# Layernorm's input for rows 1 to 3 loaded already transposed, in place of transposes on TensorE

## The chip, the cores and the metric

The kernel runs on one core of a Trainium2 chip. The metric is the device time of one execution in microseconds (us). Engines are named as in the profile: PE is TensorE (PEld its weight loads), DVE VectorE, ACT ScalarE, POOL GpSimd, and SP the engine that here only issues DMAs.

## The reference

Input x has 4 rows of 512 tokens with 1024 values each, in float32.

```python
xn = _layernorm(x)                                # (x - mean) / sqrt(var + 1e-5) over the 1024 values
q, k, v = xn @ Wq, xn @ Wk, xn @ Wv               # 16 heads of 64; rotary embedding on q and k
attn = softmax(where(causal, q @ k.T, -1e9) / sqrt(64))
s = (attn @ v) @ Wo
routing = softmax(xn @ gate_w.T, axis=1)          # 8 experts
out = (xn * (routing @ in_scale)) @ sign(weight).T * (routing @ out_scale) + bias
return x + s * silu(out)
```

## The kernel before

**Stages.** The first 770 us or so are attention; then come the output projection, the gated layer and the end. Attention works on 16 groups k = (b, g): row b of four, group g of four, a group being two units (u0 and u1) of two heads each. Groups 0 to 3 are row 0. While the softmax of one group runs, the projections of the next fill TensorE: the planning loop (L889 to L953) makes 16 `pieces` for each group, and `interleave` (L880) issues a piece and then its share of 84 projection matmuls. A float32 matmul has two records in the profile.

**Projections** take the transposed, normalized row X[b] (128 values of E by 8 chunks by 512 tokens). They follow Strassen's scheme: sums of quarters of the weights (S1 to S4, `form_w`, L288) and of X (T1 to T4, `form_x`, L311, once per row, at the end of g=3 and before its next row) are made on VectorE, seven products go through a ring of four PSUM banks (L125), and are added up on VectorE (c, v, part) and, for one term, on GpSimd (part, L388).

**One unit's chain** (names as in the profile): projection c; ScalarE swaps halves into sw (L319, L320, four instructions of 32 partitions for each of q and k), VectorE makes rot (L321), GpSimd multiplies sw by the sine (L322) and adds it to rot (L323). TensorE makes the scores sc (L525); VectorE masks and takes the maximum (L545, L548), ScalarE makes p by exp with the sum (L551), VectorE the reciprocal rs (L559), and GpSimd multiplies p by rs (L561), in eight pieces of 128, 256, 384 and 512 columns, the 128 ones last. `transpose_blocks` (L569) turns p in 32x32 blocks on VectorE (y, ten instructions, L579) and 16 DMAs on SP's queue move the blocks back to p (L589). TensorE makes the values pv (L604), and ScalarE copies them out of a bank of the ring to v (L613); a store to at_d follows (L617).

**Order.** TensorE's order is written out by hand (`manual_schedule(engines={PE})`, L61). The other engines' orders come from the tile framework's scheduler when the kernel is built, except where `tc.keep_in_program_order` fixes one; on the chip each engine takes its instructions in that order, and one that waits holds all behind it.

**Layernorm of rows 1 to 3 (b+1 while row b runs).** A row has four tiles t of 128 tokens, with tokens on partitions. `load_x` (L156) loads a tile of 512 KB: tiles 0 and 1 at piece 11 of g=1, 2 and 3 at pieces 11 and 15 of g=2. `half_statistics` (L166), `deviation` (L174) and `normalize` (L182) run at the start and at piece 3 of g=2 (tiles 0, 1) and g=3 (tiles 2, 3): two instructions of statistics (L171), their aggregate, the root on ScalarE, the reciprocal, and (x - mean) * rstd in one VectorE instruction (L187). `transpose_x` (L194) then transposes a half tile with four matmuls on TensorE (L200) at pieces 7, 8, 13 and 14, and copies the bank into X[b+1], the first half on VectorE (L204), the second on ScalarE (L206); a store of the tile to xn_d follows (L210), which the gated layer reads later. Row 0 does the same before the first group. Signs of the gated layer's weights are loaded and made (`load_sign`, `make_sign`, L679 and L706) in groups k = 5, 9, 12 and 14.

Of the kernel before, what the change touches and what calls it, by code (L numbers as in the profile page):

```python
# [9 lines left out]
F32 = mybir.dt.float32  # L10
F32R = mybir.dt.float32r
AF = mybir.ActivationFunctionType
ALU = mybir.AluOpType
# [7 lines left out]
B, S, E = 4, 512, 1024  # L21
H, D = 16, 64
NE = 8
P = 128
NT = B * S
NC = E // P
NPAIR = H // 2
NGRP = NPAIR // 2
TPB = S // P
# [13 lines left out]
def attn_gated_ffn_kernel(  # L43
    ctx: ExitStack,
    tc: tile.TileContext,
    x: bass.AP,
    wqk: bass.AP,
    wv: bass.AP,
    wo: bass.AP,
# [9 lines left out]
    nc = tc.nc  # L59
# [37 lines left out]
    for sign, base in ((1, 0), (-1, 7)):  # L97
        nc.gpsimd.affine_select(
            out=high,
            in_=high,  # L100
            compare_op=ALU.is_ge,
            fill=0.0,
            base=base,
            pattern=[[-16 * sign, 8]],
            channel_multiplier=sign,
        )
    row_kind = cp.tile([P, 3], F32, name="row_kind")


# [1 line left out]
    xn_d = dp.tile([B, TPB, P, E], F32, name="xn_d")  # L111
    at_d = dp.tile([B, TPB, P, E], F32, name="at_d")

    rt_d = dp.tile([B, TPB, 32, P], F32, name="rt_d")

    sg = {n: sgp.tile([P, E], F32R, name=f"sg{n}") for n in range(NC - 1)}
# [39 lines left out]
    def load_x(b, t):  # L156
        if b == 0:
            xt = X1[:, t, :]
        else:
            xt = xip.tile([P, E], F32, tag="x", name=f"x_{b}_{t}")  # L160
        nc.sync.dma_start(out=xt, in_=x[(b * TPB + t) * P : (b * TPB + t + 1) * P, :])
        xin[b, t] = xt
# [11 lines left out]
    def deviation(b, t):  # L174
        stats = BN[b, t]
        mv = st.tile([P, 2], F32, tag="mv", name=f"mv_{b}_{t}")
        nc.vector.bn_aggr(mv, stats)
        std = st.tile([P, 1], F32, tag="std", name=f"std_{b}_{t}")
        nc.scalar.activation(std, mv[:, 1:2], AF.Sqrt, bias=eps)
        MV[b, t] = mv, std  # L180

    def normalize(b, t):  # L182
        xt = xin[b, t]
        mv, std = MV[b, t]
        rstd = st.tile([P, 1], F32, tag="rstd", name=f"rstd_{b}_{t}")
        nc.vector.reciprocal(rstd, std)
        nc.vector.tensor_scalar(xt, xt, mv[:, 0:1], rstd, op0=ALU.subtract, op1=ALU.mult)  # L187

    def layernorm_scales(b, t):
        half_statistics(b, t, 0)  # L190
        half_statistics(b, t, 1)
        deviation(b, t)

    def transpose_x(b, t, g):  # L194
        if b not in X:
            X[b] = xp.tile([P, NC, S], F32, tag="X", name=f"X_{b}")
        tp = tp_bank(f"xtp_{b}_{t}_{g}")
        for j in range(4):
            c = 4 * g + j
            nc.tensor.transpose(tp[:, j, :], xin[b, t][:, c * P : (c + 1) * P], ident)  # L200
        dst = X[b][:, 4 * g : 4 * g + 4, t * P : (t + 1) * P]

        if (g == 0 and b > 0) or (g == 1 and (b, t) == (0, TPB - 1)):
            nc.vector.tensor_copy(dst, tp)  # L204
        else:
            nc.scalar.copy(dst, tp)  # L206
        if g == 1:

            queue = nc.scalar if (b, t) == (B - 1, TPB - 1) else nc.sync
            queue.dma_start(  # L210
                out=xn_d[b, t].rearrange("p (c q) -> p c q", c=NC),
                in_=X[b][:, :, t * P : (t + 1) * P],
            )
# [474 lines left out]
    def split_scales(dst):  # L688
        v = scales.pop(0)
        h, low, sign = (row_kind[:, n : n + 1] for n in range(3))  # L690
        pin = tc.keep_in_program_order
        if not scales_done:
            pin(nc.vector.tensor_reduce(h, high, AX.X, ALU.max))
            pin(nc.vector.tensor_scalar(low, h, -1.0, 1.0, op0=ALU.mult, op1=ALU.add))
            pin(nc.vector.tensor_scalar(sign, h, 2.0, -1.0, op0=ALU.mult, op1=ALU.add))
        scales_done.append(dst)

        pin(nc.vector.tensor_copy(dst, v))
        pin(nc.vector.tensor_scalar(v, v, low, None, op0=ALU.mult))
        pin(  # L700
            nc.vector.scalar_tensor_tensor(
                dst, dst.bitcast(F32), sign, v, op0=ALU.mult, op1=ALU.add
            )
        )
# [185 lines left out]
    for k, (b, g) in enumerate(groups):  # L890
        pieces = [[] for _ in range(9)]
        if k > 0:
            pieces, late = attention_pieces(k - 1, late)

        def at(n, piece):
            pieces[n].append(piece)


        if g == 0:
            routing = [lambda n=n: router(b, n) for n in range(3)]  # L900
            if k == 0:
                at(0, routing[0])
                at(1, lambda: (load_scales(in_scale), load_scales(out_scale)))
                at(2, routing[1])
                at(4, routing[2])
                at(5, lambda: split_scales(isc))
            else:
                if b < B - 1:
                    at(5, routing[0])
                at(8, routing[1])  # L910
                at(15, routing[2])
        elif g == 1 and b + 1 < B:

            at(11, lambda: [load_x(b + 1, t) for t in range(2)])
            if b == 0:
                at(1, lambda: split_scales(osc))
        elif g > 1 and b + 1 < B:
            t0 = 2 * (g - 2)

            layernorm_scales(b + 1, t0)  # L920
            layernorm_scales(b + 1, t0 + 1)
            normalize(b + 1, t0)
            at(3, lambda: normalize(b + 1, t0 + 1))
            for n, t, h in ((7, t0, 0), (8, t0, 1), (13, t0 + 1, 0), (14, t0 + 1, 1)):
                at(n, lambda t=t, h=h: transpose_x(b + 1, t, h))
            if g == 2:
                at(11, lambda: load_x(b + 1, 2))
                at(15, lambda: load_x(b + 1, 3))
        if k in (5, 9, 12, 14):
            n = {5: 0, 9: 2, 12: 4, 14: 6}[k]  # L930
            at(0, lambda: (load_sign(n), load_sign(n + 1)))
            at(8, lambda: make_sign(n))
            at(15, lambda: make_sign(n + 1))
        if b == B - 1:

            if g < 2:
                load_xn(g)
            if g in (1, 2):
                at(1, lambda: in_scales(g - 1, score_banks))
            if g == 3:  # L940
                z_place[0] = [xip.tile([P, E], F32, tag="x", name=f"z0_{i}") for i in range(2)]
                at(1, lambda: out_scales(0, score_banks))
        if k == 11:

            at(15, lambda: router(b + 1, 0))
        interleave(pieces, fill, 3 * 7 * 4 if k else 3 * 7 * 4 - 8)
        if g == NGRP - 1:
            for _ in fill:
                pass
            if b + 1 < B:  # L950
                for n in (3, 1, 2, 4) if b + 1 < B - 1 else (3, 2, 4, 1):
                    form_x(b + 1, n)
                fill = projections(b + 1)  # L953
# [473 lines left out]
```

## Time and profile before

| | |
|---|---|
| three runs | 1108.65, 1109.48, 1110.82 us; median 1109.48 |
| span of the profiled execution | 1108.7 us |
| granted TensorE clock, first slice to last | 0.9 or more of full speed in each of 40 |
| DMA | 163.88 MB, mean 148 GB/s |
| group starts of row 0 (g=0 to 3) | 12.5, 50.2, 92.5, 141.7 us |
| group starts of row 1 | 190.2, 238.8, 285.6, 335.6 us |
| group starts of row 2 | 383.7, 432.4, 479.1, 529.9 us |
| group starts of row 3, and their end | 578.0, 630.5, 677.2, 725.9; 772.5 us |

The groups' starts are read from the timeline of TensorE. The profile shows one execution. In a line of the groups, "out<-in" are tile names without their numbers, then the partitions and elements, the count, the busy time in us and the mean of one in ns; after the bar comes the idle time of the engine just before these instructions, and what ended most of it. A line of the timeline has start and duration in us, the engine, the line of code, the operation and how many of them; in brackets the idle time before it and who ended it. The view of waits adds up the idle time of an engine by what it waited for.

### The profile page before, as it was taken

How to read it: one execution, taken by the hardware profiler on the slowest of the kernel's cores; microseconds unless marked ns; L12 is line 12 of the kernel's file. 1: busy time of each engine (PE TensorE's matmuls, PEld its weight loads, DVE VectorE, ACT ScalarE, POOL GpSimd, SP SyncE). 2: the span in 40 equal slices, each digit the busy share in tenths (PEclk: the TensorE clock that was granted, in tenths of full speed). 3: DMA queues.
4: the chain of work that ended last, by engine and by line, in shares of the span. 5: the costliest groups of instructions: out<-in, count | busy, mean ns of one | idle time of the engine just before them, and what ended most of it. 6: DMA issues, size and time to landing. Idle time of an engine off the chain costs nothing. (4 is left out here: it accounts for less than half of the span.)

```text
span 1108.7 us, 15895 instructions
## 1 busy us (share of the span) xinstructions
PE 1087.4 (98%) x5176; PEld 790.2 (71%) x5176; DVE 870.4 (79%) x1740; ACT 461.3 (42%) x1072; POOL 518.9 (47%) x566
## 2 busy tenths in 40 slices
PE   9999999999999999999999999999999999999997
PEld 8887778777777877777788687777664545654663
DVE  7888888788988978888887887887776877567663
ACT  2452754453375445427544452655530223122220
POOL 0772645555264555526453562675552433432334
PEclk9999999999999999999999999999999999999999
DMA  9415566544556654455666445544664222431331
GB/s 323 135 69 147 149 184 189 160 137 119 166 155 187 190 154 135 121 163 158 184 183 219 140 148 142 153 125 122 179 193 171 90 93 102 148 119 54 136 114 57
DMA packets 86770, 163.88 MB, mean 148 GB/s; under 512 B 13472, under 2 KB 49056, under 8 KB 80672
## 3 DMA queue, kind: packets, MB, share of 16 engines
q1 hardware_dynamic: 80144, 152.25, 46.1%
q0 software_dynamic: 4832, 9.05, 2.4%
q10 hardware_dynamic: 1712, 1.57, 0.5%
q8 instruction: 41, 0.67, 0.3%
q14 instruction: 41, 0.34, 0.1%
HBM read 95.45 MB, written 25.43 MB: 109 GB/s over the span
## 5 line engine op out<-in xcount | busy, mean ns | idle before, releaser
L561 POOL TENSOR_SCALAR p<-p,rs 128x256 f32<-128x256 f32 (+3 forms) x256 | 183.7, 734 | 200.6 <-DVE rs L559 136.2
L551 ACT ACTIVATE p<-sc,nmx 128x256 f32<-128x256 f32 (+3 forms) x256 | 132.9, 529 | 104.8 <-DVE nmx L548 87.2
L338 PE MATMUL pj<-X,w 128*128 128x256 f32 x576 | 134.3, 382 | 1.7 <-ACT p L551 1.5
L338 PE MATMUL pj<-T,S 128*128 128x256 f32 x512 | 120.5, 385 | 8.5 <-ACT v L613 8.5
L579 DVE STREAM_TRANSPOSE y<-p 128x256 f32<-128x256 f32 x320 | 112.4, 409 | 18.3 <-POOL p L561 16.9
L322 POOL TENSOR_TENSOR sw<-sw,sin_sb 128x512 f32<-128x512 f32 x64 | 85.1, 1330 | 81.1 <-ACT sw L320 75.4
L338 PEld LDWEIGHTS pj<-X,w 128*128 128x128 f32 x576 | 108.1, 190 | 20.0 <-issue 2.9
L338 PEld LDWEIGHTS pj<-T,S 128*128 128x128 f32 x512 | 96.7, 192 | 24.8 <-ACT v L613 11.3
L319 ACT ACTIVATE sw<-c 32x512 f32<-32x512 f32 x128 | 80.3, 628 | 70.0 <-DVE c L352 68.2
L338 PE MATMUL pj<-T,w 128*128 128x256 f32 x448 | 106.6, 382 | 0.0
L548 DVE TENSOR_REDUCE nmx<-sc 128x1 f32<-128x256 f32 (+3 forms) x160 | 105.2, 683 | 1.3
L425 PE MATMUL pj<-w,X 128*128 128x256 f32 x416 | 94.6, 380 | 0.8 <-ACT p L551 0.5
L338 PEld LDWEIGHTS pj<-T,w 128*128 128x128 f32 x448 | 83.4, 190 | 15.5 <-issue 4.6
L323 POOL TENSOR_TENSOR rot<-rot,sw 128x512 f32<-128x512 f32 x64 | 90.8, 1419 | 5.0
L425 PEld LDWEIGHTS pj<-w,X 128*128 128x128 f32 x416 | 78.2, 190 | 12.7 <-ACT p L551 2.0
L545 DVE TENSOR_TENSOR sc<-sc,mask 128x256 f32<-128x256 f32 (+1 forms) x160 | 57.0, 371 | 35.3 <-PE sc L525 35.3
L320 ACT ACTIVATE sw<-c 32x512 f32<-32x512 f32 x128 | 80.4, 628 | 1.6
L425 PE MATMUL pj<-w,T 128*128 128x256 f32 x352 | 80.2, 381 | 0.0
L525 PE MATMUL sc<-rot,rot 64*128 64x128 f32 (+3 forms) x512 | 79.7, 443 | 0.3 <-DVE v L451 0.3
L604 PE MATMUL pv<-p,v 128*64 128x256 f32 (+3 forms) x512 | 76.0, 439 | 0.4 <-issue 0.4
L388 POOL TENSOR_TENSOR part<-part,part 128x256 f32<-128x256 f32 x32 | 24.7, 771 | 105.2 <-ACT part L387 102.0
L613 ACT COPY v<-pv 128x512 f32<-128x512 f32 x32 | 18.7, 585 | 131.5 <-PE pv L604 131.4
(177 smaller groups left out, 1956.9 us busy)
## 6 DMA issues: line engine op xcount, KB each, us to landing
p<-y SPq DMA_DIRECT2D x496, 80.0 KB, 2.1
w<-in_wqk SPq DMA_DIRECT2D x31, 1024.0 KB, 5.3
w<-in_wv SPq DMA_DIRECT2D x16, 1024.0 KB, 5.2
x<-in_x SPq DMA_DIRECT2D x16, 512.0 KB, 4.3
at_d<-v SPq DMA_DIRECT2D x32, 256.0 KB, 2.7
xp<-xn_d SPq DMA_DIRECT2D x16, 512.0 KB, 4.6
ap<-at_d SPq DMA_DIRECT2D x16, 512.0 KB, 5.1
xr<-in_x SPq DMA_DIRECT2D x32, 256.0 KB, 3.0
```

What stands on the lines that cost most here:

```text
L319: nc.scalar.activation(sw[r : r + 32, :], c[r + 32 : r + 64, :], AF.Copy, scale=sc)
L320: nc.scalar.activation(sw[r + 32 : r + 64, :], c[r : r + 32, :], AF.Copy, scale=sc)
L322: nc.gpsimd.tensor_tensor(sw, sw, sin_sb, op=ALU.mult)
L323: nc.gpsimd.tensor_tensor(rot, rot, sw, op=ALU.add)
L338: nc.tensor.matmul(ps, lhsT=wq[:, k, :], rhs=xq[:, k, :], start=(k == 0), stop=(k == 3))
L425: nc.tensor.matmul(ps[:, j, :], lhsT=xq[:, k, j * P : (j + 1) * P], rhs=wq[:, k, :], start=(k == 0), stop=(k == 3),)
L525: nc.tensor.matmul(head(i, h), lhsT=Q[u][r : r + D, i * P : (i + 1) * P], rhs=K[u][r : r + D, : (i + 1) * P], start=True, stop=True,)
L548: nc.vector.tensor_reduce(nmx[:, hs], v, AX.X, ALU.max, negate=True)
L551: nc.scalar.activation(pt[:, h, :], ps[h], AF.Exp, bias=nmx[:, h : h + 1], accum_out=ssum[:, h : h + 1],)
L561: nc.gpsimd.tensor_scalar(pt[:, h, :], pt[:, h, :], rs[:, h : h + 1], 1.0, op0=ALU.mult, op1=ALU.mult,)
L579: nc.vector.transpose(out[:, :, :, o : o + 32], src.rearrange("p h (b c) -> p h b c", b=4))
L604: nc.tensor.matmul(by_block[r : r + D, :, 32 * j :], lhsT=V[u][:, j, r : r + D], rhs=PT[u][:, :, o : o + 32 * (TPB - j)], start=(j == 0), ...
```

## The change

A second input xT holds x transposed on the host: for each row 128 values by 8 chunks by 512 tokens. For rows 1 to 3, X[b+1] is loaded from it straight into place, in four DMAs of 512 KB: two at piece 11 of g=1 and two at the start of g=2 (`load_xT`). The tokens' statistics still need x with tokens on partitions, so `load_x` stays, now in g=0 (last piece but three) and g=1 (piece 3), and all four tiles' statistics are made in g=1 (`token_statistics`: tiles 0 and 1 at the start, 2 at piece 8, 3 at piece 11), into one 128x32 tile sv of means and reciprocal deviations. `store_rows` turns sv in 32x32 blocks on VectorE and stores eight rows of 128 tokens with four small DMAs to sv_d in DRAM; `load_rows` loads them in g=2, repeated over all partitions, as one tile of 128x1024 (512 KB). `normalize_columns` then works on a tile of X in place, 128 partitions by 8x128: step 0 subtracts the mean's row on GpSimd (pieces 3 and 9 of g=2 and of g=3), step 1 multiplies by the deviation's row on VectorE two pieces later; both keep the program's order. The store to xn_d follows on SP's queue. Gone in rows 1 to 3: `normalize`, the 96 transposes on TensorE and their 24 copies. Row 0 is as before. Signs are made in groups 6, 10, 12 and 14 instead of 5, 9, 12 and 14, and the scratch space for the software queue's DMA descriptors is set to 8192 bytes.

The orders of the built kernels differ in these places: TensorE's is the same without the transposes. On GpSimd, in g=2, the sum part (L388) stands before the p of the unit instead of behind the first four, the first pair sw and rot before the p of 384 columns, and the second pair and the second subtraction before the p of 128 columns (before the change, these p stood between the two pairs); in g=3 the fourth subtraction stands before the p of 128 columns. On VectorE, in g=2, the small sums part and S2 stand ahead of the ten y instead of among and behind them; in g=3 a multiplication, S3, T3 and w stand between the y of the group's first unit and the next sums v.

```diff
+    sv = cp.tile([P, 32], F32, name="sv")
+    nc.gpsimd.memset(sv, 0.0)
+    sv_d = dp.tile([B, 2 * TPB, P], F32, name="sv_d")
...
-    def layernorm_scales(b, t):
+    def load_xT(b, n):
+        if n == 0:
+            X[b] = xp.tile([P, NC, S], F32, tag="X", name=f"X_{b}")
+        for c in range(4 * n, 4 * n + 4, 2):
+            nc.sync.dma_start(
+                out=X[b][:, c : c + 2, :].rearrange("p c q -> p (c q)"),
+                in_=xT[b][:, c * S : (c + 2) * S],
+            )
+    def token_statistics(b, t):
         half_statistics(b, t, 0)
         half_statistics(b, t, 1)
-        deviation(b, t)
+        two = sv[:, 2 * t : 2 * t + 2]
+        nc.vector.bn_aggr(two, BN[b, t])
+        std = st.tile([P, 1], F32, tag="std", name=f"std_{b}_{t}")
+        nc.scalar.activation(std, two[:, 1:2], AF.Sqrt, bias=eps)
+        nc.vector.reciprocal(two[:, 1:2], std)
+    def store_rows(b):
+        turned = st.tile([P, 32], F32, tag="turned", name=f"turned_{b}", bufs=1)
+        nc.vector.transpose(turned, sv)
+        for a in range(4):
+            nc.sync.dma_start(
+                out=sv_d[b][:, 32 * a : 32 * a + 32], in_=turned[32 * a : 32 * a + 2 * TPB, :]
+            )
+    ROW = {}
+    def load_rows(b):
+        ROW[b] = st.tile([P, TPB, 2, P], F32, tag="row", name=f"row_{b}", bufs=1)
+        nc.sync.dma_start(
+            out=ROW[b].rearrange("p t r q -> p (t r q)"),
+            in_=sv_d[b].rearrange("c q -> (c q)")[None, :].to_broadcast((P, 2 * TPB * P)),
+        )
+    def normalize_columns(b, t, step):
+        v = X[b][:, :, t * P : (t + 1) * P]
+        row = ROW[b][:, t, step, None, :].to_broadcast((P, NC, P))
+        if step == 0:
+            tc.keep_in_program_order(nc.gpsimd.tensor_tensor(v, v, row, op=ALU.subtract))
+            return
+        tc.keep_in_program_order(nc.vector.tensor_tensor(v, v, row, op=ALU.mult))
+        nc.sync.dma_start(out=xn_d[b, t].rearrange("p (c q) -> p c q", c=NC), in_=v)
     def transpose_x(b, t, g):
         if b not in X:
...
             nc.tensor.transpose(tp[:, j, :], xin[b, t][:, c * P : (c + 1) * P], ident)
         dst = X[b][:, 4 * g : 4 * g + 4, t * P : (t + 1) * P]
-        if (g == 0 and b > 0) or (g == 1 and (b, t) == (0, TPB - 1)):
+        if g == 1 and t == TPB - 1:
             nc.vector.tensor_copy(dst, tp)
         else:
             nc.scalar.copy(dst, tp)
         if g == 1:
-            queue = nc.scalar if (b, t) == (B - 1, TPB - 1) else nc.sync
-            queue.dma_start(
+            nc.sync.dma_start(
                 out=xn_d[b, t].rearrange("p (c q) -> p c q", c=NC),
                 in_=X[b][:, :, t * P : (t + 1) * P],
             )
...
                     at(5, routing[0])
                 at(8, routing[1])
                 at(15, routing[2])
-        elif g == 1 and b + 1 < B:
-            at(11, lambda: [load_x(b + 1, t) for t in range(2)])
-            if b == 0:
-                at(1, lambda: split_scales(osc))
-        elif g > 1 and b + 1 < B:
-            t0 = 2 * (g - 2)
-            layernorm_scales(b + 1, t0)
-            layernorm_scales(b + 1, t0 + 1)
-            normalize(b + 1, t0)
-            at(3, lambda: normalize(b + 1, t0 + 1))
-            for n, t, h in ((7, t0, 0), (8, t0, 1), (13, t0 + 1, 0), (14, t0 + 1, 1)):
-                at(n, lambda t=t, h=h: transpose_x(b + 1, t, h))
-            if g == 2:
-                at(11, lambda: load_x(b + 1, 2))
-                at(15, lambda: load_x(b + 1, 3))
-        if k in (5, 9, 12, 14):
-            n = {5: 0, 9: 2, 12: 4, 14: 6}[k]
+        if b + 1 < B:
+            last = len(pieces) - 1
+            if g == 0:
+                at(last - 3, lambda: [load_x(b + 1, t) for t in range(2)])
+            elif g == 1:
+                if b == 0:
+                    at(1, lambda: split_scales(osc))
+                token_statistics(b + 1, 0)
+                token_statistics(b + 1, 1)
+                at(3, lambda: [load_x(b + 1, t) for t in range(2, TPB)])
+                at(8, lambda: token_statistics(b + 1, 2))
+                at(11, lambda: (token_statistics(b + 1, 3), store_rows(b + 1)))
+                at(11, lambda: load_xT(b + 1, 0))
+            else:
+                t0 = 2 * (g - 2)
+                if g == 2:
+                    load_xT(b + 1, 1)
+                    load_rows(b + 1)
+                for n, t in ((3, t0), (9, t0 + 1)):
+                    at(n, lambda t=t: normalize_columns(b + 1, t, 0))
+                    at(n + 2, lambda t=t: normalize_columns(b + 1, t, 1))
+        if k in (6, 10, 12, 14):
+            n = {6: 0, 10: 2, 12: 4, 14: 6}[k]
             at(0, lambda: (load_sign(n), load_sign(n + 1)))
             at(8, lambda: make_sign(n))
             at(15, lambda: make_sign(n + 1))
...
+        "xT": np.ascontiguousarray(
+            a["hidden_states"].reshape(B, S, NC, P).transpose(0, 3, 2, 1).reshape(B, P, NC * S)
+    nc = _bacc.Bacc("TRN2", target_bir_lowering=False, num_devices=1, dynamic_dma_scratch_size=8192)
```

## The prediction

> **What bounds the kernel now.** I read the page's table of engines first, then the groups, the waits of TensorE, the stage table, and last the timeline of one group.
>
> ```profile
> PE 1087.4 (98%) x5176; PEld 790.2 (71%) x5176; DVE 870.4 (79%) x1740; ACT 461.3 (42%) x1072; POOL 518.9 (47%) x566
> ```
>
> TensorE (PE) sets the time: it is idle for some 21 of 1108.7 us, so work taken from it is gained, unless it then waits. The groups name the work that goes, and what waits where:
>
> ```profile
> L200 PE MATMUL xtp<-ident,x 128*128 128x128 f32 x128 | 18.6, 273 | 0.3 <-DVE x L187 0.3
> L338 PE MATMUL pj<-T,S 128*128 128x256 f32 x512 | 120.5, 385 | 8.5 <-ACT v L613 8.5
> L579 DVE STREAM_TRANSPOSE y<-p 128x256 f32<-128x256 f32 x320 | 112.4, 409 | 18.3 <-POOL p L561 16.9
> L311 DVE TENSOR_TENSOR T<-X 128x1024 f32<-128x1024 f32 x7 | 9.7, 1385 | 0.1
> ```
>
> The largest wait of TensorE, 8.5 us in 7 places, is for one copy on ScalarE (v, L613): the projection that follows needs that PSUM bank back. The third line says that VectorE's transposes y wait for GpSimd's normalisation p. The stage table (us from to: length, then each engine's busy time) of row 0's groups g=1, 2, 3 says how full the helpers are:
>
> ```profile
> 50.20:92.50 42.30, 42.00 (x201) 34.63 (x200) 37.30 (x69) 19.52 (x48) 24.35 (x22) 1.00 0.30 90
> 92.50:141.70 49.20, 48.00 (x249) 37.94 (x248) 40.39 (x94) 26.05 (x63) 23.94 (x31) 1.00 0.55 152
> 141.70:190.20 48.50, 48.02 (x249) 37.95 (x249) 42.39 (x91) 26.26 (x62) 22.91 (x26) 1.00 0.62 178
> ```
>
> VectorE has 5 to 9 us free in a group, GpSimd half. But order counts more than share; the timeline of row 0's g=2 shows one chain through three engines to TensorE's stall:
>
> ```profile
> 121.43 1.60 POOL L323 TENSOR_TENSOR rot<-rot,sw 128x512 f32<-128x512 f32 x1
> ...
> 123.01 1.16 POOL L561 TENSOR_SCALAR p<-p,rs 128x128 f32<-128x128 f32 x2
> ...
> 124.20 0.77 DVE L579 STREAM_TRANSPOSE y<-p 128x256 f32<-128x256 f32 x2 [0.62 <-POOL p L561]
> ...
> 129.34 0.41 DVE L352 TENSOR_TENSOR c<-pj,part 128x256 f32<-128x256 f32 x1
> ...
> 129.78 0.63 ACT L319 ACTIVATE sw<-c 32x512 f32<-32x512 f32 x1 [4.02 <-DVE c L352]
> ...
> 134.92 0.59 ACT L613 COPY v<-pv 128x512 f32<-128x512 f32 x1
> ...
> 135.56 1.13 PE L338 MATMUL pj<-T,S 128*128 128x256 f32 x4 [1.20 <-ACT v L613]
> ```
>
> Read downwards: GpSimd ends the rotary product, then the last normalisation; VectorE transposes ten blocks and forms c; ScalarE makes eight copies sw of 0.64 us and only then the copy v; TensorE goes on. No link has more than 0.1 us of slack, and the whole chain already ends 1.37 us too late. Rows 1 and 2 have the same at 329.42 and 521.9 (1.55 us each).
>
> **The change, part by part.** The order of instructions on each engine, as built, is known for both kernels; durations are those of the profile.
>
> *Transposes.* 96 of 128 go, in 24 groups of four. A group delays the next matmul by 0.44 us (started 116.80, next at 117.24; 119.40 and 119.84). 24 x 0.44 = **-10.6 us**. The busy sum, 96 x 145 ns = 13.9, counts overlapping ends twice and is the upper bound. On TensorE nothing else moves.
>
> *Copies.* 12 of ScalarE (0.584) and 12 of VectorE (0.680) go: nothing by themselves, off the path except in the chain above.
>
> *VectorE.* A tile loses the normalisation (0.885) and on average one copy (0.680), and gains a multiplication by the row, 128x1024, nearest row L311's 1.385: -0.2 us. But 6.3 us of statistics and their small steps move from g=2 and 3 into g=1, already busy for 37.3 of 42.3 us in row 0. In rows 1 and 2, one sign (two loads, and 3.2 us of VectorE) leaves g=1 for g=2 and compensates for about half.
>
> *GpSimd.* It gains 12 subtractions of 128x1024 with two inputs. No such row; 128x512 takes 1.27 alone, 2.24 at worst (61.22 us) beside VectorE. Bounds 2.5 and 4.5 us each; a floor, if the repeated row is read like a scalar, is 1.4 (the normalisation's 0.68 per 128x512, doubled). I take **2.5**, since VectorE is then waiting for the p behind it. 12 x 2.5 = 30 us would vanish in 590 us of idle GpSimd, if placed in idle time.
>
> *Where they are placed.* In g=2 the first subtraction stands in GpSimd's 16.6 us pause (97 to 114) and is free. The second stands **right ahead of** p 128x128, and the second rotary pair (sw, rot; 2.6 us) now stands ahead of p too. In return the sum "part" is made before the four p, so the first c comes 2.3 us earlier. Row 0's chain, with TensorE's start of the scores unmoved: four sw on ScalarE end at 117.7; GpSimd sw, rot to 120.35; two p to 121.9; sw, rot 122.0 to 124.6; subtraction to 127.2; first p, so y starts at 128.0 and not 124.2. The small sums now come before y, so y (ten at 0.33) and c (1.05) end at 132.35, and not 129.75. From there as before 5.8 us to TensorE: 138.2 and not 135.56, **+2.6**; the two transposes gone before it are inside this, as they only lengthen the stall, to some 4.8 us. Rows 1 and 2, worked in the same way from their own lines: +2.55 and +1.85. Sum +7.0. With the subtraction at 1.4 or 4.5 it is +3.7 or +13.
>
> *A longer stall has a second price.* After the 2.34 us wait at 620.8 the next matmuls ran at a granted clock of 0.64; after that of 1.81 us (718.8) at 1.00:
>
> ```profile
> 617.03 1.14 PE L604 MATMUL pv<-p,v 128*64 128x384 f32 x10
> 618.10 2.43 PE L525 MATMUL sc<-rot,rot 64*128 64x512 f32 x16
> 620.46 0.70 PE L338 MATMUL pj<-X,w 128*128 128x256 f32 x2
> 623.50 4.76 PE L338 MATMUL pj<-T,S 128*128 128x256 f32 x13 [2.34 <-ACT v L613]
> ...
> 623.50:628.30 4.80, 4.80 (x14) 3.91 (x15) 2.97 (x6) 4.48 (x12) 4.21 (x4) 0.64 0.49 111
> ```
>
> Eight pairs at double time cost 1.6 us. Stalls of 4.8 to 5.4 us will pay it: 3 x 1.6 = **+4.8** (bounds 0 and twice that). [...]
>
> *Later transposes.* The other two groups of each g=2 come after the stall and are gained: 3 x -0.88 = -2.6. g=2 in all: 7.0 + 4.8 - 2.6 = **+9.2**.
>
> *g=3.* The fourth subtraction again stands ahead of p 128x128 (y at 19.1 instead of 15.2 us after the scores start; 2.2 us of that is slack), and on VectorE the multiplication, S, T and w now stand between y and the sums v that the next scores need. TensorE then waits 2.15 us where it waited for nothing: net +1.25 after the two transposes ahead of it, -0.88 after. 3 x 0.37 = **+1.1**; no clock price at 2.15 (if it came, +4.8).
>
> *g=1.* Row 0: VectorE has 3.4 us more before y, and the last tile's statistics stand between y and v; the first v end at 90.3 instead of 86.2, which is TensorE's next need (it waited 0.30 for it at 86.2). **+4.1**; ends 0 and 5.7 (with a clock price). Rows 1 and 2: +0.5 each, **+1.0**.
>
> *Transfers.* 2 MB more input per row (7.5 MB in all of 163.9, queues half busy), four small stores and one 512 KB broadcast for each row: on SP's queue behind the 16 moves of p (0.63 us each to issue), landing near 104 us by the 4.6 us of the same size (xp); GpSimd wants it by 112. Nothing; beyond 8 us of delay the first subtraction waits, with four p behind it, at 1 us per us. [...] xn_d's stores leave earlier and free VectorE, which is hidden.
>
> Sum: 9.2 + 1.1 + 4.1 + 1.0 = **+15.4** on the profiled 1108.7 us = 1124.1; the median of the runs stands 0.8 above that span, so **1125 us**.
>
> **Rivals.**
> *The whole gain arrives (faster).* GpSimd's and VectorE's additions all end before anyone needs them; then -10.6, 1099 us (1096 by the upper bound). For it: GpSimd is idle for half the span and the pauses are long. Against: the chain has no slack, and the subtraction is in it by order. It decides if the chain is no later than now, that is if y starts by some 125.4 in row 0, which needs 2.6 us from somewhere: a subtraction near 1.4 us and a rotary pair that starts about 1.4 us earlier than I have it.
> *Half.* The subtraction costs 1.4 to 2, the clock stays at 1.00 after the stalls, as it did after that of 1.81 us, and row 0's g=1 hides at least in part: +9.2 falls to about +2, total +3 to +8: 1112 to 1117.
> *Balance.* Chain +1 us a row, transposes pay for it: within 2.2 us of before. (0.2%, 2.2 us, is about what a measurement of this kernel can tell from no change.)
> *Worse.* GpSimd and VectorE slow each other: 4.5 us a subtraction, +6 in g=2, +4.8 clock in g=3, 1.6 in g=1: 1134 to 1140. For it: rot took 2.14 beside VectorE at 59 us against 1.27 alone. [...]
> *The change does not do what it says:* the order of TensorE shows the 96 transposes gone, so this can only be the row trip coming late (the margin of 8 us above); put into "worse".
>
> **How the numbers follow.** Chains late as priced, 1117 to 1134: 0.54, and the forecast. Half: 0.09. Balance: 0.06. Whole gain: 0.25. Worse: 0.06. So faster 0.25, same 0.06, slower 0.69. The range takes in the whole gain at 1098, and the priced chains at their upper bounds, 1134; the likeliest case's own range is 1117 to 1134.
>
> **What the profile would show.** L200 at 32 instructions. Subtractions on GpSimd of about 2.5 us, the second of each g=2 ending just before p 128x128. The wait "y <- POOL p" growing from 16.9 us by 3 to 4 us for each g=2, and TensorE's wait for the copy v from 8.5 to some 20 us, in stalls of 4 to 5 us with a granted clock below 0.8 after each. If that wait is no longer than now, the chain was wrong and the time is near 1099. If the stalls are there but the clock is 1.00, take off 5 us. A wait of GpSimd for a DMA ahead of the subtraction would mean that the row trip is late.

## The result, and the profile after

The changed kernel takes 1123.79 us (median of 4 runs, 1122.52 to 1124.13), against 1109.07 for the kernel before in the same comparison: a ratio of 1.0131, with a 95% interval of 1.0116 to 1.0145. It is slower, by 14.7 us; the forecast was 1125.0. The profiled execution has a span of 1122.2 us.

The engines and two groups of the page, to be laid beside those of before:

```profile
PE 1086.2 (97%) x5080; PEld 787.8 (70%) x5080; DVE 855.6 (76%) x1731; ACT 455.5 (41%) x1060; POOL 545.2 (49%) x579
...
L380 PE MATMUL pj<-T,S 128*128 128x256 f32 x512 | 125.1, 399 | 16.1 <-ACT v L655 16.1
L621 DVE STREAM_TRANSPOSE y<-p 128x256 f32<-128x256 f32 x320 | 111.6, 408 | 33.5 <-POOL p L603 33.3
```

TensorE has 96 instructions fewer but is busy for only 1.2 us less: most of what the transposes gave back went into matmuls that were there before, the projections pj<-T,S at a longer mean (399 ns, and 385 before) and the scores (82.7 us busy, and 79.7 before). Its wait for the copy v doubled from 8.5 to 16.1 us, and VectorE's wait for GpSimd's p from 16.9 to 33.3. The full list of groups has the lines that the change made or shrank:

```profile
L233 POOL TENSOR_TENSOR X<-X,row 128x1024 f32<-128x1024 f32 x12 | 31.2, 2596 | 9.6 <-DMA row<-sv_d 9.6
...
L235 DVE TENSOR_TENSOR X<-X,row 128x1024 f32<-128x1024 f32 x12 | 14.5, 1208 | 0.0
...
L244 PE MATMUL xtp<-ident,x 128*128 128x128 f32 x32 | 4.2, 274 | 0.3 <-DVE x L191 0.3
```

A subtraction costs GpSimd 2.60 us on average (median 2.35), a multiplication VectorE 1.21. GpSimd waited 9.6 us in all for the rows to land, ahead of first subtractions only; these stand in its pause, and nobody waited for them.

Where the time came from, by groups (length after minus before, us, from the starts of the groups' matmuls):

| | g=0 | g=1 | g=2 | g=3 |
|---|---|---|---|---|
| row 0 | -0.01 | +3.05 | +4.45 | -0.57 |
| row 1 | +0.07 | -0.50 | +4.64 | -0.24 |
| row 2 | +0.07 | -0.49 | +4.11 | +0.77 |
| row 3 | -1.62 | 0.00 | 0.00 | +0.01 |

So 13.2 of the 13.5 us stand in the three g=2. The timeline of row 0's g=2 after the change, with the same links as the one of before:

```profile
127.04 1.26 POOL L365 TENSOR_TENSOR rot<-rot,sw 128x512 f32<-128x512 f32 x1
...
128.26 2.34 POOL L233 TENSOR_TENSOR X<-X,row 128x1024 f32<-128x1024 f32 x1
...
130.58 0.72 POOL L603 TENSOR_SCALAR p<-p,rs 128x128 f32<-128x128 f32 x2
...
131.34 3.38 DVE L621 STREAM_TRANSPOSE y<-p 128x256 f32<-128x256 f32 x10 [5.67 <-POOL p L603]
...
135.22 0.41 DVE L394 TENSOR_TENSOR c<-pj,part 128x256 f32<-128x256 f32 x1
...
135.66 0.63 ACT L361 ACTIVATE sw<-c 32x512 f32<-32x512 f32 x1 [9.01 <-DVE c L394]
...
140.80 0.58 ACT L655 COPY v<-pv 128x512 f32<-128x512 f32 x1
...
141.44 5.92 PE L380 MATMUL pj<-T,S 128*128 128x256 f32 x16 [4.43 <-ACT v L655]
```

The second subtraction ends where p begins; y, c, the eight sw and v follow without a gap; TensorE stands for 4.43 us, and its next 16 matmuls take 5.92 us instead of 3.72. The stage table of the stretches behind this stall and behind row 1's (last but two: the granted clock) says why:

```profile
141.44:147.40 5.96, 5.96 (x17) 4.90 (x18) 2.23 (x7) 3.09 (x11) 3.35 (x5) 0.62 0.58 138
338.46:345.00 6.54, 6.54 (x18) 5.33 (x19) 2.99 (x8) 4.30 (x14) 4.62 (x7) 0.58 0.52 126
```

### The profile page after: what moved, and what is told of

Its sections match the earlier page's. It is cut to its first block, busy times and chain, and to the rows that moved or that the text cites. A ratio compares the mean times of both kernels' runs of the same rounds, so it can differ in the third digit from the quotient of the medians.

```text
span 1122.2 us, 15734 instructions
## 1 busy us (share of the span) xinstructions
PE 1086.2 (97%) x5080; PEld 787.8 (70%) x5080; DVE 855.6 (76%) x1731; ACT 455.5 (41%) x1060; POOL 545.2 (49%) x579
## 5 line engine op out<-in xcount | busy, mean ns | idle before, releaser
L603 POOL TENSOR_SCALAR p<-p,rs 128x256 f32<-128x256 f32 (+3 forms) x256 | 177.2, 708 | 152.6 <-DVE rs L601 105.4
L380 PE MATMUL pj<-T,S 128*128 128x256 f32 x512 | 125.1, 399 | 16.1 <-ACT v L655 16.1
L621 DVE STREAM_TRANSPOSE y<-p 128x256 f32<-128x256 f32 x320 | 111.6, 408 | 33.5 <-POOL p L603 33.3
L380 PEld LDWEIGHTS pj<-T,S 128*128 128x128 f32 x512 | 102.0, 201 | 34.6 <-ACT v L655 19.2
L380 PEld LDWEIGHTS pj<-T,w 128*128 128x128 f32 x448 | 83.9, 190 | 15.4 <-issue 4.6
L567 PE MATMUL sc<-rot,rot 64*128 64x128 f32 (+3 forms) x512 | 82.7, 445 | 6.4 <-DVE v L493 3.5
L467 PEld LDWEIGHTS pj<-w,T 128*128 128x128 f32 x352 | 66.5, 190 | 10.6 <-issue 2.0
```

The lines of the kernel that those rows point to most:

```text
L380: nc.tensor.matmul(ps, lhsT=wq[:, k, :], rhs=xq[:, k, :], start=(k == 0), stop=(k == 3))
L467: nc.tensor.matmul(ps[:, j, :], lhsT=xq[:, k, j * P : (j + 1) * P], rhs=wq[:, k, :], start=(k == 0), stop=(k == 3),)
L567: nc.tensor.matmul(head(i, h), lhsT=Q[u][r : r + D, i * P : (i + 1) * P], rhs=K[u][r : r + D, : (i + 1) * P], start=True, stop=True,)
L603: nc.gpsimd.tensor_scalar(pt[:, h, :], pt[:, h, :], rs[:, h : h + 1], 1.0, op0=ALU.mult, op1=ALU.mult,)
L621: nc.vector.transpose(out[:, :, :, o : o + 32], src.rearrange("p h (b c) -> p h b c", b=4))
```

## The experiments

Theory **order**: the loss is made by what stands ahead of p 128x128 in GpSimd's queue in g=2 (the second subtraction and the second rotary pair); the chain behind p is late, TensorE stalls, and its clock is lower behind the stall (0.62 and 0.58 above). Rival **load**: the added work itself (statistics in g=1, roots with their table loads, 30 us on GpSimd, two engines at work side by side) slows things wherever it stands. In each comparison the kernel before took 1109.6 to 1110.5 us.

**Later subtraction** (e1). The second subtraction of each group (in g=3 that is the fourth) and its multiplication are given out two pieces later; in g=2 the subtraction so lands behind p.

```diff
-                for n, t in ((3, t0), (9, t0 + 1)):
+                for n, t in ((3, t0), (11, t0 + 1)):
```

> The changed kernel with the second subtraction of each group two pieces later: on GpSimd it now stands behind p 128x128 instead of ahead of it; nothing else moves there. Theory (order): the stalls of TensorE for the copy v shrink by one subtraction, 2.35 us, from 4.4, 3.8 and 3.4 to some 2.1, 1.5 and 1.0 us, and the low clock behind them (2.2 to 2.9 us each) goes; with up to 2 us from g=3 in all 13 to 16 us: 1107 to 1111. Rival (load): what costs is the added work and traffic itself, wherever it stands: 1122 to 1125. Rival (clock only): the stalls shrink but the clock still falls behind them: 1114 to 1117.

Measured: 1116.85 us, ratio 1.0063 (1.0046 to 1.0079). Half the loss went, not all of it: a miss for "order" as I had stated it. The number is that of the third case, in which the clock still falls; it did, but the stalls too stayed longer than any case had them. TensorE's timeline at row 1's stall:

```profile
333.08 5.41 PE L380 MATMUL pj<-T,S 128*128 128x256 f32 x16 [3.46 <-ACT v L655]
```

The waits in the three g=2 fell from 4.6, 5.2 and 4.7 us (two waits added up) to 2.90, 3.46 and 3.44, as the chain moved by 2.31 us; but 2.90 us is still a stall, and behind it too the 16 matmuls took 5.41 us and not 3.72. And the g=3 stayed long (47.19, 47.19 and 48.44 us): there TensorE waits 0.6, 0.6 and 1.9 us for rs. GpSimd isn't what is late (behind the fourth subtraction, at 179.71 in row 0, it is idle for 10.48 us); VectorE is. Its sum S at 180.51 takes 2.10 us beside that subtraction, against 0.65 in e2, and the multiplication stands ahead of v and rs.

**No subtraction** (e2). All 12 are left out, so the token means stay in X.

```diff
         if step == 0:
-            tc.keep_in_program_order(nc.gpsimd.tensor_tensor(v, v, row, op=ALU.subtract))
             return
```

> The changed kernel without the 12 subtractions of the mean on GpSimd (rows 1 to 3 are only scaled); the order of all else is the same. Order theory: within 1.5 us of e1_subtract_later, 1106 to 1111, since a subtraction that holds nobody up costs nothing. If the subtraction also slows VectorE or GpSimd by its mere presence: 3 us or more below e1. Load theory (statistics, multiplication, traffic): 1120 or more.

Measured: 1111.20 us, 1.0013 (1.0004 to 1.0023). The g=2 stalls are those of e1, 2.90, 3.45 and 3.44 us, with no subtraction anywhere; the g=3 fall to 45.98, 45.98 and 46.57. The time is 5.65 us below e1, where "order" had within 1.5 and a cost of the subtraction's mere presence 3 or more. What falls is mostly g=3, by 1.2 to 1.9 us a row, where e1's fourth subtraction held up S on VectorE; so its presence does cost there, by where it stands, and e11 shows the same subtractions in a place where they cost nothing. So the subtraction's 2.3 us was one part of the lateness in g=2. The other part must stand in the chain without it; the second rotary pair ahead of p is the candidate, which e5 and e12 try.

**Values twice** (e3). The matmuls of the values that come before g=2's stall are done twice in rows 0 to 2 (`times` is 2 there; 2.15 us more of TensorE each time), to fill the stall and keep the clock.

```diff
-        for j in range(TPB):
+        for j in list(range(TPB)) * times:
```

> The changed kernel in which TensorE makes the second unit's values (16 matmuls, 2.4 us) twice in g=2 of rows 0 to 2, just ahead of the stalls; orders of the other engines are unchanged. If idle time of TensorE lowers its clock: the copy v comes no later, the stalls shrink from 4.4, 3.8 and 3.4 to about 2.0, 1.4 and 1.0 us, and the matmuls behind them run at full clock: 6 to 8 us less, 1115.5 to 1118, with more work on the engine that sets the time. If the low clock has another cause: 1123 to 1125. If TensorE's work counts in full: 1131.

Measured: 1123.31 us, 1.0126 (1.0111 to 1.0141). A miss in the sum; the three stalls tell it apart:

```profile
141.84 3.72 PE L380 MATMUL pj<-T,S 128*128 128x256 f32 x16 [3.04 <-ACT v L655]
...
337.33 5.41 PE L380 MATMUL pj<-T,S 128*128 128x256 f32 x16 [4.24 <-ACT v L655]
...
534.53 6.04 PE L380 MATMUL pj<-T,S 128*128 128x256 f32 x16 [4.25 <-ACT v L655]
```

In row 0 of this profile the extra work shortened the stall to 3.04 us, the clock held (3.72 us for 16 matmuls), and the group took 51.46 instead of 53.66 us, with more work in it. (One execution: after a wait of the same length in e4 ten matmuls took 4.64 us and not 2.43.) In rows 1 and 2 the second pass first filled another wait (1.37 us, of the scores for c) and pushed v behind one more sw: the stall grew, and the clock fell. Some 6.5 us of extra TensorE work cost nothing in the sum: in g=2 of the changed kernel, TensorE doesn't set the time.

**Late p in the kernel before** (e4). The kernel before, with one more subtraction of 128x1024 on a spare tile, right ahead of p 128x128 in g=2 of rows 0 to 2 (the first unit numbered with group 1 gets its last p there). Of the change it has only the smaller scratch space for descriptors.

```diff
+            late = i == 0 and u[0] < B - 1 and u[1:] == (1, 0)
+            if late:
+                tc.keep_in_program_order(nc.gpsimd.tensor_tensor(
+                    spare, spare, rs[:, 0:1].to_broadcast((P, E)), op=ALU.subtract
+                ))
```

> The kernel before, with one thing added: a subtraction of 128x1024 on GpSimd, on a spare tile that nobody reads, right ahead of p 128x128 in g=2 of rows 0 to 2 (three in all), and a tile of 4 KB in the place of descriptor space. Theory (the chain from p to the copy v has no slack): each stall grows by 2.35 to 3.5 to 3.9 us, and the clock falls behind it: 3 x (2.35 + 1.6 to 2.5) = 12 to 15 us more, 1121 to 1124. If the chain has slack: 1109 to 1112. If the stalls grow and the clock stays: 1116 to 1117.

Measured: 1117.24 us, 1.0075 (1.0056 to 1.0094): three GpSimd instructions, 7 us of an engine that is idle for half the span, cost 7.6 us. That is below the forecast of 1121 to 1124; the profiled execution is the slowest of the four (1120.64 us at a mean clock of 0.988; the others 1115.8 to 1117.9 at 0.991 to 0.994), so the full price of the clock was not paid in each. Two views of its timeline, GpSimd in row 0 and TensorE's stall:

```profile
123.01 2.34 POOL L564 TENSOR_TENSOR spare<-spare,rs 128x1024 f32<-128x1024 f32 x1
125.33 0.71 POOL L568 TENSOR_SCALAR p<-p,rs 128x128 f32<-128x128 f32 x2
...
137.43 4.64 PE L340 MATMUL pj<-T,S 128*128 128x256 f32 x10 [3.04 <-ACT v L622]
```

p moved by 2.29 us (from 123.01 to 125.33) and TensorE's resumption by only 1.84 (from 135.56 to 137.43), both less the 0.03 by which this run's g=2 starts later: some 0.45 us of slack had been in the chain. The clock's price in this profile was 2.2 us (10 matmuls in 4.64, not 2.43). "Load" can't explain this run.

**p first** (e5). e1, and GpSimd's order in g=2 is pinned: p 128x128 ahead of the second rotary pair, as before the change. (Before the change only p 128x128 stood between the two pairs; p of 384 columns, at 117.59 us, stood ahead of both. Here it stays behind the first pair.)

```diff
+        pin = tc.keep_in_program_order if m == 0 and u[1] > 1 else lambda i: i
-        nc.gpsimd.tensor_tensor(sw, sw, sin_sb, op=ALU.mult)
+        pin(nc.gpsimd.tensor_tensor(sw, sw, sin_sb, op=ALU.mult))
...
+                pin = tc.keep_in_program_order if u[2] == 0 and i in (0, 2) and u[1] in (1, 2) else lambda i: i
-                nc.gpsimd.tensor_scalar(
+                pin(nc.gpsimd.tensor_scalar(
```

> As e1_subtract_later, and in g=2 p 128x128 now stands ahead of the second rotary pair (sw, rot) on GpSimd, as in the kernel before; nothing else moves on GpSimd or VectorE. Order theory: y starts 2.5 us earlier, the stalls of 2.90, 3.46 and 3.44 us fall below 1.1 us and the low clock behind them (1.7 to 2.9 us each) goes: 3 x 2.5 + 5 to 7 below e1's 1116.9 = 1102 to 1105, faster than the kernel before. Load theory (statistics, multiplication, traffic): 1115 to 1118.

Measured: 1112.75 us, 1.0015 (1.0002 to 1.0029), a miss. The eleven runs lie in two clumps, five at 1108.33 to 1109.16 us and six at 1112.75 to 1114.39; the profile is of the second. Row 0 did what was expected: its stall is 0.31 us and its g=2 46.57 us long. Rows 1 and 2 kept stalls of 3.42 and 3.43. The timeline of row 1 shows a new cause:

```profile
319.77 2.37 POOL L233 TENSOR_TENSOR X<-X,row 128x1024 f32<-128x1024 f32 x1
319.88 2.81 DVE L330 TENSOR_TENSOR S<-w 128x512 f32<-128x512 f32 x1
```

The weight sum S on VectorE, elsewhere 0.69 us, starts beside the subtraction and ends 0.55 us after it; y and c wait behind S. So "load" has a part of the truth: not the amount of work but this sum and a subtraction at one moment.

**One root** (e6). e5 with a single root and reciprocal for the four tiles, at the end of g=1, instead of four (table loads on ScalarE fall from 19 to 13).

```diff
+        var = sv[:, 0 : 2 * TPB].rearrange("p (t r) -> p t r", r=2)[:, :, 1]
+        nc.scalar.activation(std, var, AF.Sqrt, bias=eps)
+        nc.vector.reciprocal(var, std)
```

> As e5, and the roots of a row's four tiles are taken in one instruction on ScalarE at the end of g=1 instead of four, so that fewer activation tables are loaded there. If the wait of 1.27 us in row 0's g=1 (TensorE for p, behind a table load of 1.28 us) comes from the root of tile 1: 1 to 2 us below e5. If the table load only moves to another place on the path: within 0.7 us of e5.

Measured: 1112.83 us, 1.003 (1.002 to 1.0039): no gain from the table loads shows in the sum. Row 0's g=1 got longer (48.05 us; one wait of 2.49 us for v, and behind it 26 matmuls in 8.58 us, where the same 26 at 185.47 took 5.88).

**No statistics** (e7). The changed kernel without the statistics; sv stays zero, so X is multiplied by zero.

```diff
-        half_statistics(b, t, 0)
-        half_statistics(b, t, 1)
-        nc.vector.bn_aggr(two, BN[b, t])
-        nc.scalar.activation(std, two[:, 1:2], AF.Sqrt, bias=eps)
-        nc.vector.reciprocal(two[:, 1:2], std)
```

> The changed kernel without the token statistics of rows 1 to 3 (no statistics, roots or reciprocals; the rows are filled with zeros and X is multiplied by them). On GpSimd, in g=1 only, part and p 128x128 trade places. Order theory: row 0's g=1 gives back its 3.05 us, g=2 and g=3 keep theirs: 1119.5 to 1122. Load theory (VectorE's and ScalarE's added work in g=1 is the main cause): below 1113.

Measured: 1122.53 us, 1.0116 (1.0102 to 1.0130). "Load" would have this near 1113; it falls. It lies just above the 1119.5 to 1122 of "order", since row 0's g=1 gave back less than the 3.05 us counted on. That group shrank only from 45.38 to 44.56 us (42.33 before the change); the wait behind a table load is gone, but waits for part (0.93) and v (1.07) are there.

**Transposes gone alone** (e8). The kernel before, with X of rows 1 to 3 loaded from xT and neither transposes nor copies in those rows; what the layernorm computes isn't put into X.

```diff
-        for j in range(4):
+        for j in range(4 if b == 0 else 0):
...
+            at(11, lambda: load_xT(b + 1, 0))
```

> The kernel before with one part of the change alone: X of rows 1 to 3 is loaded from the transposed input, and their transposes and copies are left out; x is still normalized with tokens on partitions, but X is not. No work is added on GpSimd. The 24 groups of transposes are worth 10.6 us on TensorE; of these, 6 groups (2.6 us) lie ahead of the stalls of g=2, which then grow by as much if the chain to the copy v stays where it is: 1100.5 to 1102.5. If the chain moves up with them: 1098.5 to 1100.

Measured: 1101.45 us, 0.9924 (0.9912 to 0.9937): a hit, but not for the reason given. In the profile the groups g=2 and g=3 of rows 0 to 2 shrink by 11.0 us together: the 10.6 us of the transposes are real, and the old stalls swallow little of them (1.70, 1.07 and 1.07 us, against 1.20, 1.38 and 1.39 before). What is lost again stands elsewhere: row 0's g=1 is 1.06 us longer, and behind the attention TensorE waits 2.72 us, at 812.21, for z_t.

**No collision** (e9). e5's order, with the second subtraction of g=2 at piece 14 and its multiplication at 15.

```diff
+                for n, m, t in ((3, 5, t0), (14 if g == 2 else 11, 15 if g == 2 else 13, t0 + 1)):
```

> As e5_p_first, with the second subtraction of g=2 alone moved on, behind the p of the next unit, so that it no longer runs beside the sum S that VectorE makes between y and c (2.81 us beside the subtraction in rows 1 and 2 of e5, 0.68 us elsewhere); its multiplication moves on with it. If the two engines hold each other up: S takes 0.7 us again, the stalls of rows 1 and 2 fall from 3.42 to about 1.3 us, the low clock behind them (2.8 us each) goes, and the time is 1103 to 1108, below the kernel before. If S was long for another cause (the weights it reads, for one): the stalls stay at 3.4 us, 1109 to 1114.

Measured: 1107.78 us, 0.9978 (0.9967 to 0.9989): a hit, though the runs lie in two clumps on either side of that median (last section); the profile is of the faster one. S and the stall in row 1:

```profile
320.71 0.65 DVE L330 TENSOR_TENSOR S<-w 128x512 f32<-128x512 f32 x1
...
327.48 3.72 PE L381 MATMUL pj<-T,S 128*128 128x256 f32 x16 [1.29 <-ACT v L657]
```

S is back at 0.65 us, the stalls are 0.35, 1.29 and 1.28 us, and the clock holds (3.72 us for 16 matmuls behind each). What is left is in g=3 (48.47, 49.53 and 50.80 us).

**Fourth late too** (e10). e9, and the fourth subtraction put off as well.

```diff
+                for n, m, t in ((3, 5, t0), (14, 15, t0 + 1)):
```

> As e9_no_collision, with the fourth subtraction (g=3) moved on in the same way. TensorE's waits of 0.63 us (rows 1, 2) and 1.9 us (row 3) at the end of g=3 in e5, for the reciprocal rs, go if the fourth subtraction and its multiplication cause them: 1 to 3 us below e9. If the sums T of X, which come right behind it, are late for the next row's projections: 1 us or more above e9.

Measured: 1117.22 us, 1.0071 (1.0059 to 1.0083). TensorE's timeline at the start of rows 1 and 3:

```profile
198.55 5.33 PE L381 MATMUL pj<-T,S 128*128 128x256 f32 x16 [2.91 <-DVE T L353]
...
586.50 3.62 PE L673 MATMUL lg<-X,gw 128*32 128x128 f32 x58 [6.25 <-DVE X L235]
```

The next row needs its X at once: its sums T, and for row 3 the routing, which waited 6.25 us. So the fourth subtraction can't be put off; it has to come earlier.

**Both in the pause** (e11). The changed kernel with both subtractions of a group at piece 3, in GpSimd's pause (n is the subtraction's piece, m the multiplication's). Nothing else moves on GpSimd.

```diff
-                for n, t in ((3, t0), (9, t0 + 1)):
+                for n, m, t in ((3, 5, t0), (3, 11, t0 + 1)):
```

> The changed kernel with both subtractions of a group at piece 3, in GpSimd's pause of some 10 us ahead of the sum part; on GpSimd nothing else moves, so p 128x128 still stands behind the second rotary pair. On VectorE the fourth multiplication now stands ahead of y in g=3. If a subtraction costs nothing where GpSimd is idle: like e2_no_subtract, within 1.5 us of 1111.2. If it slows what VectorE does at that time, or the rows are not there yet: 1114 or more.

Measured: 1111.22 us, 1.0015 (1.0006 to 1.0024). A hit: the same 31 us of subtractions, given out earlier, cost what leaving them out did (1111.20). The stalls of the rotary pair are still there, in row 1:

```profile
331.05 6.47 PE L380 MATMUL pj<-T,S 128*128 128x256 f32 x16 [3.46 <-ACT v L655]
```

**Both in the pause, p first** (e12). e11 with e5's pinned order; all of the computation is in it.

```diff
+                for n, m, t in ((3, 5, t0), (3, 11, t0 + 1)):
...
+        pin = tc.keep_in_program_order if m == 0 and u[1] > 1 else lambda i: i
```

> As e11_both_in_pause, and in g=2 p 128x128 stands ahead of the second rotary pair, as in e5 and e9. Stalls for the copy v of 0.4 us (row 0) and 1.3 us (rows 1, 2) as in e9, no low clock, and of e9's waits in g=3 (0.9 to 1.1 us for v, 0.6 to 1.9 us for rs) only a part: 1101 to 1105, the fastest with all of the work in it. If g=3 is bound by VectorE's multiplications themselves: as e9, 1106 to 1109.

Measured: **1097.11 us** (5 runs, 1095.20 to 1099.33), 0.9891 (0.9875 to 0.9906): faster than both kernels, and than I expected. GpSimd's timeline in row 0's g=2, and TensorE's stall there:

```profile
102.59 4.68 POOL L233 TENSOR_TENSOR X<-X,row 128x1024 f32<-128x1024 f32 x2 [1.20 <-DMA row<-sv_d]
115.34 0.72 POOL L431 TENSOR_TENSOR part<-part,part 128x256 f32<-128x256 f32 x1 [8.07 <-ACT part L430]
...
124.40 2.71 POOL L605 TENSOR_SCALAR p<-p,rs 128x384 f32<-128x384 f32 x4
127.08 1.27 POOL L365 TENSOR_TENSOR sw<-sw,sin_sb 128x512 f32<-128x512 f32 x1
...
137.25 3.72 PE L381 MATMUL pj<-T,S 128*128 128x256 f32 x16 [0.32 <-ACT v L657]
```

Two subtractions, 4.68 us, fit into the pause with 8 us to spare; the pieces of p (two of 384 and two of 128 columns, one line here) end before the rotary pair; the stall is 0.32 us. The three g=2 take 46.58, 47.52 and 47.52 us, and the g=3 45.98, 45.98 and 46.63.

## Why the prediction was right, point by point

The direction, and in g=2 the place and the mechanism, came out as forecast. That the sum came so near is in part luck: g=2 was put 4.1 us too low and all else 6.0 us too high. The terms, in us:

| step | predicted | measured |
|---|---|---|
| g=2: the chain makes TensorE resume later | +7.0 | +8.1 (3.14, 2.86, 2.10) |
| g=2: lower clock after the stalls | +4.8 | +7.8 (2.20, 2.67, 2.90) |
| g=2: transposes behind the stall | -2.6 | -2.6 |
| g=3 | +1.1 | -0.04 |
| g=1, row 0 | +4.1 | +3.05 |
| g=1, rows 1 and 2 | +1.0 | -1.0 |
| row 3, g=0 | 0 | -1.6 |
| start and rest | 0 | -0.2 |
| sum, on the span | +15.4 | +13.5 |

- **The chain** was right link by link: p starts at 130.58, y ends near 134.7 and TensorE goes on at 141.44, in a group that starts 2.74 us later than before. The subtraction was taken at 2.5 us and took 2.34 there. e1 and e2 split the lateness: 2.3 us are the subtraction's, the rest is the rotary pair's. Both were in the working; that taking away only the first would leave a stall was not. VectorE's wait for p was foreseen to grow by 9 to 12 us and grew by 16; TensorE's waits for v came to 16.1 and, for c ahead of it, 2.9 us, against some 20. "No slack" was a little too strict (0.45 us by e4). (Row 2's stall before the change ends at 523.69 us, not near 521.9 as the working has it; its length there is right.)
- **The clock** was the term most undersized. I priced 1.6 us an event from one row; the three stalls cost 2.2 to 2.9.
- **g=3.** The predicted wait for v came out at 0.7 us rather than 2.15, and the transposes gone paid for it.
- **g=1 of row 0.** Nearly the size, not the cause. I had all 4.1 us from late sums v; the profile has 1.36 us for v and 1.27 for p, behind a table load on ScalarE (1.28 us at 67.95) that follows a root and that I had not counted. Without any statistics (e7) only 0.8 us came back. In e7 VectorE's work of this group already starts late, and e8, with nothing added to VectorE there, is 1.06 us longer in the same group; in e8 a sum c on VectorE waits 1.46 us for GpSimd's part at the end of g=0. What makes this start late is **not settled**.
- **g=1 of rows 1 and 2.** The sign was wrong: the second unit's scores, stretched to 3.06 us before by a wait among them, took 2.43.
- **Row 3.** Its stall of 2.32 us was there as before, but this time the clock didn't fall (16 matmuls in 3.72 us, and 5.41 before). Other profiles with this stall show either (see below): luck, and not a gain of the change.
- **From span to median.** I added 0.8 us, since the median of before stood that far above its profiled span; here it is 1.6. That hid 0.8 of the 1.9 us that the terms were too high.
- **The rivals.** "The whole gain" named its condition: y in time. e12 fulfils it with the same work, and gains 1.1% on before. The two steps are nearly equal: placement of the subtractions 12.6 us (from the changed kernel to e11, by medians), the rotary pair behind p 14.1 (from e11 to e12). "Worse", engines that slow each other, did not decide in the changed kernel, but e5 shows it: S took 2.81 us beside a subtraction, and 0.69 elsewhere.

## What to carry to other kernels

An engine that is idle for half the span can still cost more than all the work put on it is worth (in e4, 7 us on GpSimd cost 7.6): ask of each added instruction not how long it is but who is queued right behind it, and place it in a pause that the timeline shows. After mending one link, look again at the whole chain and at what the moved piece now runs beside: two of my expectations failed because the next cause (the rotary pair in e1, the collision with S in e5) was a link away, and e10 ran into a third (the next row's T). And price a stall of the bounding engine twice, once as waiting and once as a lower clock after it (here 2.2 to 2.9 us behind waits of 3.4 to 4.4).

## What the runs showed of the hardware

- **Behind a short stall TensorE was often slower.** Over the 14 profiles (both kernels and the experiments), 16 projection matmuls after a wait of up to 2.09 us always took 3.72 us. After row 3's wait of 2.32 to 2.37 us, the same place in every kernel, they took 5.1 to 5.4 us in 9 profiles and 3.72 in 5; after waits of 2.88 to 3.04 us they took 5.1 to 5.4 us (in e4, ten matmuls 4.6) in 6 of 7 places and 3.72 in one; after 3.2 us or more they took 5.1 to 6.7 us, or ten matmuls 4.6, in all 20. A shorter wait could do as much in another place: ahead of row 3's first projections, six matmuls behind a wait of 1.88 to 1.89 us took 2.45 to 2.64 us in three profiles (e1, e5, e6) and 1.53 in one (e9). In the records of the granted clock, for the kernel before and for the changed one, it is 1.00 or 0.50, and changes 5 and 9 times, each time a multiple of 3.41 us after the profile's first change. During the attention it fell once before the change, for 3.41 us, and three times after it, for 6.83, 6.83 and 10.24; in the 3.41 us ahead of these falls matmuls covered 1.07 us, and 1.33, 1.02 and 2.05. Row 3's stall, by stretches of this length, before the change and after it (length; busy time of PE, PEld, DVE, ACT, POOL; granted clock, DMA):

```profile
620.99:624.40 3.41, 1.07 (x5) 0.83 (x5) 3.38 (x8) 3.33 (x7) 1.92 (x2) 1.00 0.55 124
624.40:627.81 3.41, 3.41 (x10) 2.67 (x9) 1.58 (x5) 3.37 (x11) 2.90 (x3) 0.50 0.45 101
...
633.99:637.40 3.41, 2.31 (x16) 1.10 (x12) 3.41 (x8) 2.45 (x4) 0.00 (x0) 1.00 0.52 116
637.40:640.81 3.41, 2.19 (x10) 1.96 (x11) 2.24 (x5) 3.31 (x7) 2.75 (x3) 1.00 0.55 124
```

Before, the wait of 2.34 us lies in one such stretch, matmuls cover 1.07 us of it, and the clock falls at its end; after, the 2.32 us are split over two, with 2.31 and 2.19 us covered, and it holds. These are two profiles, and what makes the clock fall is not settled by them. The same kernel can show either: e9's 12 runs lie at 1105.7 to 1106.1 us, with mean clocks of 0.997 and 0.998, and at 1109.5 to 1109.8, with 0.993 to 0.995.

- **Sums of weights on VectorE and subtractions on GpSimd held each other up.** In e5 the sum S from two quarters took 0.69 us (median of 64) and 2.81 beside a subtraction of 2.37 us; the sum S<-w,S took 0.68 (median of 32) and 1.90 when it started 1.01 us into a subtraction of 2.36 (131.12 and 130.11 us). Both ended 0.55 us after the subtraction. The reverse, in the changed kernel:

```profile
161.63 1.96 DVE L330 TENSOR_TENSOR w<-w 128x1024 f32<-128x1024 f32 x1
...
162.47 3.34 POOL L233 TENSOR_TENSOR X<-X,row 128x1024 f32<-128x1024 f32 x1
```

The three of its 12 subtractions that started during such a w of 128x1024 took 3.33 to 3.34 us, and ended 2.2 us after it; the other nine took 2.34 to 2.37. (The one that e4 adds in row 0, whose second input is one value for each partition, started during a w of 128x512 and took its 2.34 us.) In each of the three pairs the later instruction lost about what was left of the earlier one when it started: 2.12 of 2.26 us, 1.22 of 1.35, 0.99 of 1.12. That looks like waiting, and not like sharing. Not all work on VectorE was held up: beside subtractions of the changed kernel ten transposes y took 3.38 us (at 299.73), as without one (at 131.34), and a sum c, which has two inputs, 0.42 (at 102.86), and 0.41 without one (at 135.22).

- **Extra work ahead of a stall cost nothing here.** In e3, 2.15 us more of matmuls ahead of each of three stalls left the time of the kernel as it was (1123.31 us, and 1123.79 without them).
